# A two-step graph attention layer: the first step's guess kept as a logarithm, its last arithmetic moved from VectorE to ScalarE and GpSimd

## The chip, the cores and the metric

The kernel runs on one core of a Trainium2 chip. A core has five engines with queues of their own: TensorE (PE in the profile, with its weight loads as PEld), VectorE (DVE), ScalarE (ACT), GpSimd (POOL) and SyncE (SP), which here only issues transfers. The metric is the device time of one launch in microseconds.

## The reference, cut to what matters

`x` is 3327 x 256, `adj` is a sparse 3327 x 3327 matrix (about 0.12% of its entries and the diagonal), all float32.

```python
def _top_p_attention(X, W1, W2, W3):
    logits = (X @ W1.T @ W2.T) @ (X @ W3.T).T
    probs = softmax(logits, axis=-1)
    # sort each row downward; keep an entry while the sum before it is under 0.9
    keep_sorted = cs - sp < TOP_P
    A = probs * mask
    return A / A.sum(-1)

h = relu(layernorm(x))
R = rownorm(adj + I)
Z, Xf, Xa = 0, h, h
for n in range(2):
    A = _top_p_attention(Xa, W1, W2, W3)
    Xf = R @ Xf
    Xa = A @ Xa
    Z = Z + Xf @ U1[n].T + Xa @ U2[n].T
out = x + layernorm(h + Z) * ln_g + ln_b
```

So each of the two steps forms 3327 rows of 3327 attention weights, cuts from each row the smallest entries that make up the last tenth of its sum, and multiplies what is left by the node features. Beside it runs the sparse product with `R`.

## The kernel before

**Tiles and slots.** The rows are split into 26 tiles of 128. Each step is a loop over slots, one tile each (`for i in range(-1, NT + 2)`); a slot has seven parts (`PARTS`). What is issued in each part is written out by hand as strings in `PLAN`, `BEGIN`, `OPEN` and `LAST`: each letter advances one generator to its next `yield`. At the end dependencies are added that hold PE, ACT, DVE and POOL to the order of the program text, so the text is the queue of each engine.

**The way of a tile through the first step.** `weights` (letters w, q) makes a row block of logits on PE and its exponentials on ACT (lines 600 to 610). `measured_once` (letter m) guesses, for each row, a value a little above the cut: a few operations on one column per row on ACT and POOL (lines 620 to 646), two scans of all 3328 entries on ACT (line 633: a sum of Relu and a sum of Sign against a first guess), then seven one-column operations on ACT (lines 653 to 659) and five on DVE (lines 662 to 666), the last of which writes the guess, column 16. `settle` (letters d, c) then takes one DVE pass over the row block that keeps what is under the guess (line 724, "the w pass" below), searches the largest 40 of these with MAX8 and MATCH_REPLACE8 (lines 732 to 751), and takes a second DVE pass that writes zeros under the cut found (line 761, "the e pass"). `Sums` transposes the block on PE (line 810), copies it from PSUM on ACT (line 812) and multiplies it by the features on PE (line 824). Column 16 only has to be close: `prove` checks afterwards that each row's cut is exact, and where one isn't, the whole layer is computed again by `search_graph_layer`, a slower kernel in the same program.

**The sparse product.** `listed` (letter a) reads `adj` and finds for each row block which of the column blocks hold anything (lines 854 to 863); the first four of a row go into `index` directly, the rest are counted on DVE into `over` (line 866) and packed: `packed` (letter p) multiplies the counts by a triangular matrix on PE (line 876), copies the result on ACT (line 877) and makes a 128 x 128 selection of zeros and ones with two DVE operations (lines 880 and 881); `gathered` (letter h) multiplies by it (line 887) and writes the fifth index (lines 889 to 895). With these indices POOL issues ten indirect transfers per tile, five of `adj` blocks (line 901) and five of feature rows (line 922). Letter g issues one of the ten; each is made to follow the ACT instruction that stands last before it in the text. `spread` (letter s) is the product on PE (line 930). `first_end` (letter e) ends a tile's first step: a transposition, a product with `U2`, and on POOL the sum of line 947, `sv`.

**Queues around the change.** POOL's queue in a slot of the first step holds, in this order from the w pass on: the rest of the feature gathers (line 922), `index` of line 895, five operations of `project` (lines 541 to 545), in every other slot line 502, one `adj` gather and the sum of line 907, lines 643 to 646 of the guess, then line 922, four of line 901 with `index` of line 864 among them, and the sum of line 947. DVE's queue holds the w pass, the MAX8 work with the reductions of `listed` in between, lines 880 and 881, the e pass, line 763, line 894, lines 662 to 666, line 538, and the next w pass.

Of the kernel before, what the change touches and what calls it, by code (L numbers as in the profile page):

```python
# [9 lines left out]
F32 = mybir.dt.float32  # L10
# [3 lines left out]
AF = mybir.ActivationFunctionType  # L14
ALU = mybir.AluOpType
# [3 lines left out]
P = 128  # L19
# [4 lines left out]
NP = NT * P  # L24
# [288 lines left out]
BIG = 1.0e30  # L313
# [3 lines left out]
ROUNDS = (5, 5)  # L317
PG = (0.72168716, 3.51308980, -3.48705157)
PK = (3.57528079, -2.54929187, 0.86603878)
OFFSET = (18.0, 24.0)  # L320
TOPK = 8 * max(ROUNDS)
LNY = 0.25 * math.log(0.72)

SQG, SQK = ((c[0], c[1] / (2 * c[0]), c[2] - c[1] ** 2 / (4 * c[0])) for c in (PG, PK))
# [12 lines left out]
DIRECT = 4  # L337
LIST = 16
# [7 lines left out]
def guess_graph_layer(ctx, tc, x, adj, w1t, w2t, w3t, u1t, u2t, ln_g, ln_b, out, flag):  # L346
    nc = tc.nc

    const = ctx.enter_context(tc.tile_pool(name="const", bufs=1))
# [6 lines left out]
    small = ctx.enter_context(tc.tile_pool(name="small", bufs=4))  # L356
# [5 lines left out]
    V, G, S, PE = nc.vector, nc.gpsimd, nc.scalar, nc.tensor  # L362

    rows_of = lambda t: min(P, N - t * P)
    valid = lambda t: 0 <= t < NT
# [44 lines left out]
    for k, c in enumerate((-0.5, 0.5, -1.0, -0.5)):  # L410
        G.memset(half[:, k : k + 1], c)
    law = const.tile([P, 7, NT], F32, tag="law", name="law")
    one = const.tile([P, 8], F32, tag="one", name="one")
    for k, c in enumerate((1.0, -1.0, 5.0e-4, SQG[1], SQK[1], math.log(10.0), LNY, 1.0e-12)):
        G.memset(one[:, k : k + 1], c)
    of_s = const.tile([P, 4], F32, tag="of_s", name="of_s")
    for k, c in enumerate((SQG[0], SQG[2], -SQK[0], -SQK[2])):
# [14 lines left out]
    place = const.tile([P, P], F32, tag="place", name="place")  # L432
# [5 lines left out]
    lists = const.tile([P, NT, LIST + 1], F32, tag="lists", name="lists")  # L438
    over = const.tile([P, NT], F32, tag="over", name="over")
# [188 lines left out]
    def con(k):  # L628
        return one[:, k : k + 1]
# [5 lines left out]
    def measured_once(r):  # L635
        e, ms = r["e"], r["ms"]


        col = guessed(r, small.tile([P, 17], F32, tag="g", name="g"))
        S.activation(col(4), col(2), AF.Square, bias=con(4))  # L640
        S.activation(col(11), col(4), AF.Identity, scale=ms(5), bias=ms(6))
        S.activation(col(1), col(0), AF.Exp, scale=-1.0, bias=con(5))
        G.tensor_scalar(col(7), col(9), 0.5, None, ALU.mult)
        G.tensor_scalar(col(8), col(9), 0.5 * NP, None, ALU.mult)
        G.tensor_scalar(col(5), col(1), OFFSET[0], None, ALU.mult)
        G.tensor_scalar(col(10), col(9), col(5), 1.0, ALU.mult, ALU.add)
        yield
        oa = small.tile([P, 3], F32, tag="oa", name="oa")
        through(e, AF.Relu, col(9), -1.0, oa[:, 0:1])
        yield  # L650
        through(e, AF.Sign, col(9), -1.0, oa[:, 1:2])
        yield
        S.activation(col(3), oa[:, 0:1], AF.Identity, scale=-1.0, bias=col(8))
        S.activation(col(4), oa[:, 1:2], AF.Relu, scale=col(7), bias=col(3))
        S.activation(col(6), col(4), AF.Ln, scale=col(1), bias=con(2))
        S.activation(col(3), col(4), AF.Square, scale=col(1), bias=con(1))
        S.activation(col(3), col(3), AF.Ln, scale=0.5, bias=col(10))
        S.activation(col(3), col(3), AF.Identity, scale=-1.0, bias=col(6))
        S.activation(col(3), col(3), AF.Exp, scale=col(11))
        yield  # L660

        V.tensor_scalar(col(5), oa[:, 1:2], NP - 31.0, BIG, ALU.is_gt, ALU.mult)
        V.tensor_scalar(col(6), col(4), col(1), 0.35, ALU.mult, ALU.is_lt)
        V.scalar_tensor_tensor(col(5), col(6), BIG, col(5), ALU.mult, ALU.add)
        V.tensor_scalar(col(3), col(3), 1.0e20, col(9), ALU.min, ALU.mult)
        V.tensor_tensor(col(16), col(3), col(5), ALU.add)

    def measured_twice(r):
        e, ms = r["e"], r["ms"]
# [6 lines left out]
        G.tensor_scalar(col(11), col(11), ms(5), ms(6), ALU.mult, ALU.add)  # L676
        G.tensor_scalar(col(5), col(1), OFFSET[1], None, ALU.mult)
        G.tensor_scalar(col(7), col(3), ms(3), ms(8), ALU.mult, ALU.add)
# [33 lines left out]
    def measured(step, r):  # L712
        return measured_twice(r) if step else measured_once(r)
# [123 lines left out]
    def listed():  # L837
        pieces = [(t, j0, min(size, NT - j0)) for t in range(NT) for size in (HALF if t < HALVES else AD,)
                  for j0 in range(0, NT, size)]

        def asked(t, j0, n):
            at = (roomy[(2 * t + j0 // HALF) % 4] if t < HALVES else
                  adjp.tile([P, AD, P], F32, tag="at", name="at", bufs=2))
            nc.sync.dma_start(at[:, :n], adj[t, :, j0 : j0 + n, :])
            return at

        ahead = asked(*pieces[0])
        for k, (t, j0, n) in enumerate(pieces):
            at = ahead
            if k + 1 < len(pieces):  # L850
                ahead = asked(*pieces[k + 1])
            if j0 == 0:
                fm = small.tile([P, NT], F32, tag="fm", name="fm", bufs=2)
            V.tensor_reduce(fm[:, j0 : j0 + n], at[:, :n], AX.X, ALU.max, apply_absolute_value=True)  # L854
            if j0 + n < NT:
                yield
                continue
            V.scalar_tensor_tensor(fm, fm, 0.0, back, ALU.is_gt, ALU.mult)
            V.memset(fm[:, t : t + 1], 0.0)
            ls = lists[:, t, :]  # L860
            V.max(ls[:, :8], fm)
            V.match_replace(fm, ls[:, :8], fm, 0.0)
            V.max(ls[:, 8:LIST], fm)
            G.tensor_scalar(index[:, t, :DIRECT], ls[:, :DIRECT], -1.0, float(NONE), ALU.mult, ALU.add)
            of = small.tile([P, LIST], F32, tag="of", name="of", bufs=2)
            V.tensor_scalar(of[:, DIRECT:], ls[:, DIRECT:LIST], 0.0, None, ALU.is_gt, ALU.add,
                            accum_out=over[:, t : t + 1])
            done.append(t)
            yield

    def packed(t):

        assert t in done
        ls, ov = lists[:, t, :], over[:, t : t + 1]
        pb = ps_t.tile([P, 4, P], F32, tag="pt", name="pb")
        PE.matmul(pb[:, 0, :1], upto, ov, start=True, stop=True)
        S.copy(ls[:, LIST:], pb[:, 0, :1])
        yield
        ohs[t] = oh = small.tile([P, P], F32, tag="oh", name="oh", bufs=2)
        V.tensor_scalar(oh, place, ov, ls[:, LIST:], ALU.subtract, ALU.is_lt)  # L880
        V.scalar_tensor_tensor(oh, place, ls[:, LIST:], oh, ALU.is_ge, ALU.mult)

    def gathered(t):
        oh = ohs.pop(t)
        ls, n = lists[:, t, :], LIST - DIRECT
        po = ps_t.tile([P, 4, P], F32, tag="pt", name="po")
        PE.matmul(po[:, 0, : n + 1], oh, ls[:, DIRECT:], start=True, stop=True)
        lo = small.tile([P, n], F32, tag="lo", name="lo", bufs=2)
        S.copy(lo, po[:, 0, :n])
        nth = small.tile([P, 1], F32, tag="nth", name="nth")  # L890
        S.activation(nth, po[:, 0, n : n + 1], AF.Identity, scale=-1.0, bias=part)
        yield
        of = small.tile([P, LIST], F32, tag="of", name="of", bufs=2)
        V.scalar_tensor_tensor(of[:, :n], place[:, :n], nth, lo, ALU.is_equal, ALU.mult, accum_out=nth)
        G.tensor_scalar(index[:, t, DIRECT:], nth, -1.0, float(NONE), ALU.mult, ALU.add)

    def adjacent(t):
# [83 lines left out]
        V.tensor_copy(flag, pf[:1, 0, :1])  # L981

    own_of = {}
    live, ohs, acs, xgs, done, early = {}, {}, {}, {}, [], {}
    none = iter(())

    def run(work, n=99):
# [42 lines left out]
    for q in range(HALF + 5):  # L1030
        if 0 <= q - 3 < HALF:
            k, pk = q - 3, made.pop(q - 3)
# [17 lines left out]
        if 0 <= q - 2 < HALF:  # L1050
            k, pt = q - 2, turned.pop(q - 2)
# [10 lines left out]
        if 0 <= q - 1 < HALF:  # L1062
            k, rn = q - 1, scaled.pop(q - 1)
            pt = ps_t.tile([P, 4, P], F32, tag="pt", name="pt")
            for h in range(2):
                t = 2 * k + h
# [4 lines left out]
        if 0 <= q - 4 < HALF and 2 * (q - 4) in COUNTED:  # L1071
            k = q - 4
# [54 lines left out]
    def refetch(t):  # L1127
# [6 lines left out]

    PLAN = (("gmdsssa", "gmcdsssa", "edawwpg", "gmsdga", "gmspdea", "ohgdawwqg", "gehmgq"),
            ("llcmssg", "lnmsg", "lwwnfdgg", "lcmdsss", "fdsmwqdf", "llmd", "lmwfdg"))

    LAST = {NT - 1: ("cfss", "cn", "nd", "sss", "fddddddsf", "f", ""), NT: ("c", "", "", "ff", "ff", "fv", "f"),  # L1140
            NT + 1: ("fv", "f", "", "", "f", "f", "f")}
    BEGIN = {-1: ("mba", "mmbba", "mwwbbaa", "bmwwb", "", "", ""),
             0: ("mdbb", "mcdbb", "medbwwbp", "mdbb", "gmpdbwwb", "hgdbgbq", "hgq"),
             1: ("ggmdsssbb", "gmcdgsssbb", "gedbwwbp", "bmsdg", "gmpdeg", "hgdwwqg", "hgemgqo"),
             2: ("gmdsssa", "gmcdsssga", "gedawwpg", "gmsdga", "gmspdea", "ohgdawwqg", "gehmgq")}
    OPEN = {-1: ("llcmss", "lnms", "lwwnfd", "lcmdsssggggg", "fmgdswqdf", "llmdf", "lmwfdm"),
            0: ("cmssggg", "nms", "wwnfd", "cmdsss", "fdsmgwqdf", "mdf", "mwd"),
            1: ("cmss", "nms", "wwnfd", "cmdsssgggg", "fdsmwqdf", "mgd", "mwfdg")}
# [9 lines left out]
    for step in range(2):  # L1158
        sums = Sums(step, live, xw if step else x0, AHEAD[step])

        for i in range(-1, NT + 2):
# [4 lines left out]
            if step == 1 and i == -1:  # L1166
# [6 lines left out]
                c=work["d"],  # L1173
# [25 lines left out]
            for k in range(PARTS):  # L1199
                g = PARTS * (i - 1) + k - LATE[step]  # L1200
                summing = valid(g // PARTS)
                if step and valid((g + AHEAD[1]) // PARTS):
                    sums.turn(g + (k == 2), min(i, NT - 1))
                for c in ({**OPEN, **LAST} if step else BEGIN).get(i, PLAN[step])[k]:
                    at = len(trace)
# [76 lines left out]
```

## Time and profile before

| | us |
|---|---|
| median of 3 runs | 1366.73 |
| lowest and highest of the runs | 1366.65 to 1367.74 |
| the profiled execution, its time | 1366.65 |
| its span (first to last instruction) | 1364.9 |
| beginning, up to the first slots | 0 to 136 |
| slots of the first step | 136 to about 680 |
| between the steps | 680 to 760 |
| slots of the second step | 760 to 1365 |

The span is 1.75 us shorter than the execution's time; the granted TensorE clock is 0.984 of full speed over the whole span, and 1.00 in the slots of the first step from 209 to 618 us. In the page, a group's line gives line, engine, operation, output and inputs, shapes and count, then the busy time of the group, the mean of one in ns, and the idle time before them with what ended it. In the timeline each line is a start, a duration, an engine and an instruction.

### The profile page before, as it was taken

How to read it: one execution, taken by the hardware profiler on the slowest of the kernel's cores; microseconds unless marked ns; L12 is line 12 of the kernel's file. 1: busy time of each engine (PE TensorE's matmuls, PEld its weight loads, DVE VectorE, ACT ScalarE, POOL GpSimd, SP SyncE). 2: the span in 40 equal slices, each digit the busy share in tenths (PEclk: the TensorE clock that was granted, in tenths of full speed). 3: DMA queues.
4: the chain of work that ended last, by engine and by line, in shares of the span. 5: the costliest groups of instructions: out<-in, count | busy, mean ns of one | idle time of the engine just before them, and what ended most of it. 6: DMA issues, size and time to landing. Idle time of an engine off the chain costs nothing.

```text
span 1364.9 us, 22101 instructions
## 1 busy us (share of the span) xinstructions
PE 1267.0 (93%) x6495; PEld 973.5 (71%) x6495; DVE 1150.7 (84%) x3455; ACT 1072.4 (79%) x2342; POOL 1048.0 (77%) x1425
## 2 busy tenths in 40 slices
PE   5989999999999999999999499999998999999985
PEld 4535778777787877778786277767676767676775
DVE  6877999999999999999973788787878787878793
ACT  5466788889888888888844898898979898989851
POOL 5215888888888888888872788888888888888872
PEclk9989999999999999999999699999999999999998
DMA  8734454454545455453532222212221312122200
GB/s 293 223 117 136 132 162 130 142 158 129 160 133 148 138 144 150 138 160 107 146 89 85 62 75 65 78 61 80 66 74 50 90 50 90 58 82 65 75 24 23
DMA packets 92642, 149.77 MB, mean 110 GB/s; under 512 B 15425, under 2 KB 59072, under 8 KB 92512
## 3 DMA queue, kind: packets, MB, share of 16 engines
q1 hardware_dynamic: 75056, 105.37, 24.6%
q0 software_dynamic: 16640, 42.69, 11.9%
q8 instruction: 54, 0.88, 0.3%
q14 instruction: 76, 0.62, 0.1%
q10 hardware_dynamic: 816, 0.20, 0.1%
HBM read 120.93 MB, written 27.28 MB: 109 GB/s over the span
## 4 chain that ended last, share of the span: by engine, by line
DVE 47%; PE 24%; POOL 16%; ACT 6%; issue 5%; DMA 1%; POOLq 0%; SPq 0%; DVEq 0%; ACTq 0%
DVE e L761 9%; DVE cand L732 8%; PE pa L824 7%; DVE w L724 6%; POOL xg L922 6%; PE pl L600 5%; DVE fm L854 5%; DVE bb L739 3%; PE pt L810 3%; DVE cand L741 3%; PE pr L930 3%; ACT ja L633 3%; PE pz L1012 2%; DVE x L761 2%; POOL s L970 1%
## 5 line engine op out<-in xcount | busy, mean ns | idle before, releaser
L824 PE MATMUL pa<-xw,eT 128*128 128x256 f32 x1352 | 322.6, 383 | 4.2 <-DVE s L954 2.3
L633 ACT ACTIVATE ja<-e,g 128x3328 uint8<-128x3328 f32 x106 | 325.9, 3074 | 0.1
L824 PE MATMUL pa<-x,eT 128*128 128x256 f32 x1352 | 322.0, 379 | 0.0
L824 PEld LDWEIGHTS pa<-xw,eT 128*128 128x128 f32 x1352 | 249.8, 190 | 53.3 <-issue 14.4
L824 PEld LDWEIGHTS pa<-x,eT 128*128 128x128 f32 x1352 | 242.8, 190 | 25.5
L732 DVE MAX8 cand<-w 128x8 f32<-128x168 f32 (+1 forms) x1040 | 253.4, 317 | 0.0
L922 POOL DMA_INDIRECT xg<-bx,index x130 | 202.2, 1555 | 50.8 <-issue 23.4
L812 ACT COPY eT<-pt 128x512 f32<-128x512 f32 (+1 forms) x364 | 200.2, 557 | 43.0 <-PE pt L810 42.8
L810 PE MATMUL pt<-ident,e 128*128 128x128 f32 x1144 | 176.2, 276 | 29.9 <-DVE e L761 18.3
L901 POOL DMA_INDIRECT ac<-in_adj,index x130 | 148.9, 1145 | 59.0 <-ACT e L1018 16.5
L810 PEld LDWEIGHTS pt<-ident,e 128*128 128x128 f32 x1144 | 139.3, 144 | 73.6 <-issue 44.3
L724 DVE SCALAR_TENSOR_TENSOR w<-e,g 128x3328 f32<-128x3328 f32 x44 | 163.7, 3720 | 2.6 <-ACT g L709 2.5
L922 POOL DMA_INDIRECT xg<-vx,index x130 | 134.6, 1035 | 40.6 <-issue 24.6
L761 DVE SCALAR_TENSOR_TENSOR e<-e,rec 128x3328 f32<-128x3328 f32 x40 | 151.7, 3792 | 0.6
L930 PE MATMUL pr<-xg,ac 128*128 128x257 f32 (+1 forms) x520 | 140.5, 394 | 8.2 <-DVE s L1120 6.5
L604 ACT ACTIVATE e<-pl 128x832 f32<-128x832 f32 x132 | 113.1, 861 | 28.6 <-PE pl L600 25.8
L930 PEld LDWEIGHTS pr<-xg,ac 128*128 128x128 f32 x520 | 93.7, 194 | 34.7 <-issue 15.0
L600 PE MATMUL pl<-both,qT 64*128 64x416 f32 x416 | 93.0, 546 | 7.7 <-ACT e L604 4.3
L600 PE MATMUL pl<-after,qT 64*128 64x416 f32 x416 | 97.2, 562 | 0.2 <-ACT e L604 0.2
L739 DVE MAX8 bb<-cand 128x8 f32<-128x160 f32 x260 | 84.3, 324 | 5.5
L466 POOL TENSOR_TENSOR rstd<-rstd,half 128x1 f32<-128x1 f32 x26 | 84.1, 3236 | 2.2
L854 DVE TENSOR_REDUCE fm<-at 128x4 f32<-128x512 f32 (+1 forms) x133 | 84.3, 634 | 0.6 <-DMA at<-in_adj 0.6
(258 smaller groups left out, 2140.9 us busy)
## 6 DMA issues: line engine op xcount, KB each, us to landing
at<-in_adj SPq DMA_DIRECT2D x114, 256.0 KB
cx<-ac SPq DMA_DIRECT2D x26, 384.0 KB
ac<-cx SPq DMA_DIRECT2D x26, 384.0 KB
wide<-in_adj SPq DMA_DIRECT2D x8, 832.0 KB
e<-in_adj SPq DMA_DIRECT2D x6, 832.0 KB
own<-bx SPq DMA_DIRECT2D x26, 128.5 KB
x<-in_x SPq DMA_DIRECT2D x13, 256.0 KB
xr<-in_x SPq DMA_DIRECT2D x26, 128.0 KB
```

The lines of the kernel that those rows point to most:

```text
L600: PE.matmul(pl[:, a, :wd], qT[p, :], keys_of(step, a).rearrange("p a b -> p (a b)")[:, c : c + wd], start=True, stop=True)
L633: S.activation(ja, e, f, bias=guess, scale=sign, accum_out=total)
L724: V.scalar_tensor_tensor(w, e, col(16), e, ALU.is_lt, ALU.mult, accum_out=d2)
L732: V.max(cand[:, 8 * s : 8 * s + 8], w[:, s * SEG : min(NP, (s + 1) * SEG)])
L761: V.scalar_tensor_tensor(e, e, at(1), e, ALU.is_ge, ALU.mult, accum_out=ra)
L810: PE.transpose(pt[:, j, :], e[:, (j0 + j) * P : (j0 + j + 1) * P], ident)
L812: S.copy(eT[:, :w, :], pt[:, :w, :])
L824: PE.matmul(self.pa, eT[:, c - 4 * k, :], self.xa[:, j, :], start=c == 0, stop=c == NT - 1)
L854: V.tensor_reduce(fm[:, j0 : j0 + n], at[:, :n], AX.X, ALU.max, apply_absolute_value=True)
L901: G.indirect_dma_start(out=ac[:, k, :], out_offset=None, in_=rows, in_offset=bass.IndirectOffsetOnAxis(ap=index[:, t, k : k + 1], axis=0), ...
L922: G.indirect_dma_start(out=xg[:, k, :w], out_offset=None, in_=rows, in_offset=bass.IndirectOffsetOnAxis(ap=index[:, t, k : k + 1], axis=0))
L930: PE.matmul(pr[:, :w], ac[:, k, :], own if k == KT - 1 else xg[:, k, :w], start=k == 0, stop=k == KT - 1)
```

## The change

The change touches the first step's guess and the packing of indices; the numbers of search rounds stay (5, 5).

- The guess of the first step is worked out as a logarithm. Four POOL operations on one column are added in the first part of `measured_once` (a sign change, two for a constant less the logarithm of the first guess, 0.035 of the row's sum). On ACT a Square leaves the seven operations after the scans, and two of the seven, now a Relu and an Exp, stand behind three DVE operations in a fifth part of the generator, which is issued in part 5 of the slot, ahead of the e pass, where before five DVE operations stood at the slot's end. The two guards that before added 1e30 to the guess now take 60 from the term under the Relu. The constant in the logarithm goes from 18 to 19.
- The count of the blocks beyond the first four moves from a DVE operation in `listed` to a Sign with a sum on ACT, in a new function `counted`, with two new one-column POOL operations. It is issued two tiles ahead, in `gathered`.
- In `packed`, one of two DVE operations on 128 x 128 remains; a one-column Identity and a 128 x 128 Square on ACT are added.

```diff
-OFFSET = (18.0, 24.0)
+OFFSET = (19.0, 24.0)
@@ measured_once
         S.activation(col(1), col(0), AF.Exp, scale=-1.0, bias=con(5))
+        G.tensor_scalar(col(11), col(11), -1.0, None, ALU.mult)
         G.tensor_scalar(col(7), col(9), 0.5, None, ALU.mult)
         G.tensor_scalar(col(8), col(9), 0.5 * NP, None, ALU.mult)
         G.tensor_scalar(col(5), col(1), OFFSET[0], None, ALU.mult)
         G.tensor_scalar(col(10), col(9), col(5), 1.0, ALU.mult, ALU.add)
+        G.tensor_scalar(col(12), col(3), ms(3), ms(8), ALU.mult, ALU.add)
+        G.tensor_scalar(col(12), col(12), -1.0, 80.0, ALU.mult, ALU.add)
+        G.tensor_scalar(col(13), r["Z"], 0.035, None, ALU.mult)
         yield
...
         S.activation(col(6), col(4), AF.Ln, scale=col(1), bias=con(2))
-        S.activation(col(3), col(4), AF.Square, scale=col(1), bias=con(1))
-        S.activation(col(3), col(3), AF.Ln, scale=0.5, bias=col(10))
-        S.activation(col(3), col(3), AF.Identity, scale=-1.0, bias=col(6))
-        S.activation(col(3), col(3), AF.Exp, scale=col(11))
-        yield
-
-        V.tensor_scalar(col(5), oa[:, 1:2], NP - 31.0, BIG, ALU.is_gt, ALU.mult)
-        V.tensor_scalar(col(6), col(4), col(1), 0.35, ALU.mult, ALU.is_lt)
-        V.scalar_tensor_tensor(col(5), col(6), BIG, col(5), ALU.mult, ALU.add)
-        V.tensor_scalar(col(3), col(3), 1.0e20, col(9), ALU.min, ALU.mult)
-        V.tensor_tensor(col(16), col(3), col(5), ALU.add)
+        S.activation(col(10), col(10), AF.Ln)
+        S.activation(col(10), col(10), AF.Identity, scale=-1.0, bias=col(6))
+        yield
+        V.tensor_scalar(col(5), oa[:, 1:2], NP - 31.0, 60.0, ALU.is_gt, ALU.mult)
+        V.tensor_scalar(col(14), col(4), col(13), 60.0, ALU.is_lt, ALU.mult)
+        V.scalar_tensor_tensor(col(12), col(12), col(5), col(14), ALU.subtract, ALU.subtract)
+        S.activation(col(10), col(10), AF.Relu, scale=col(11), bias=col(12))
+        S.activation(col(16), col(10), AF.Exp, scale=-1.0, bias=con(8))
@@ listed
-            of = small.tile([P, LIST], F32, tag="of", name="of", bufs=2)
-            V.tensor_scalar(of[:, DIRECT:], ls[:, DIRECT:LIST], 0.0, None, ALU.is_gt, ALU.add,
-                            accum_out=over[:, t : t + 1])
+    def counted(t):
+
+        if t not in done or t in nhs:
+            return
+        of = small.tile([P, LIST], F32, tag="of", name="of", bufs=2)
+        ov = over[:, t : t + 1]
+        S.activation(of[:, DIRECT:], lists[:, t, DIRECT:LIST], AF.Sign, accum_out=ov)
+        nhs[t] = nh = small.tile([P, 3], F32, tag="nh", name="nh", bufs=4)
+        G.tensor_scalar(nh[:, 0:1], ov, -0.5, 0.5, ALU.mult, ALU.add)
+        G.tensor_scalar(nh[:, 1:2], ov, ov, 0.25, ALU.mult, ALU.mult)
@@ packed
         S.copy(ls[:, LIST:], pb[:, 0, :1])
-        yield
+        S.activation(nh[:, 2:3], pb[:, 0, :1], AF.Identity, scale=-1.0, bias=nh[:, 0:1])
         ohs[t] = oh = small.tile([P, P], F32, tag="oh", name="oh", bufs=2)
-        V.tensor_scalar(oh, place, ov, ls[:, LIST:], ALU.subtract, ALU.is_lt)
-        V.scalar_tensor_tensor(oh, place, ls[:, LIST:], oh, ALU.is_ge, ALU.mult)
+        S.activation(oh, place, AF.Square, bias=nh[:, 2:3])
+        yield
+        V.tensor_scalar(oh, oh, nh[:, 1:2], None, ALU.is_lt)
@@ gathered
         V.scalar_tensor_tensor(of[:, :n], place[:, :n], nth, lo, ALU.is_equal, ALU.mult, accum_out=nth)
+        if valid(t + 2):
+            counted(t + 2)
         G.tensor_scalar(index[:, t, DIRECT:], nth, -1.0, float(NONE), ALU.mult, ALU.add)
@@ the plan of the first step, part 5 (likewise in BEGIN)
-    PLAN = (("gmdsssa", "gmcdsssa", "edawwpg", "gmsdga", "gmspdea", "ohgdawwqg", "gehmgq"),
+    PLAN = (("gmdsssa", "gmcdsssa", "edawwpg", "gmsdga", "gmspdea", "ohgmdawwqg", "gehmgq"),
```

More of the change, by code (lines that the diff above doesn't have):

```diff
@@ L412, in guess_graph_layer @@
     law = const.tile([P, 7, NT], F32, tag="law", name="law")
-    one = const.tile([P, 8], F32, tag="one", name="one")
-    for k, c in enumerate((1.0, -1.0, 5.0e-4, SQG[1], SQK[1], math.log(10.0), LNY, 1.0e-12)):
+    one = const.tile([P, 9], F32, tag="one", name="one")
+    for k, c in enumerate((1.0, -1.0, 5.0e-4, SQG[1], SQK[1], math.log(10.0), LNY, 1.0e-12, 80.0)):
         G.memset(one[:, k : k + 1], c)
@@ L864, in listed @@
             G.tensor_scalar(index[:, t, :DIRECT], ls[:, :DIRECT], -1.0, float(NONE), ALU.mult, ALU.add)
-            of = small.tile([P, LIST], F32, tag="of", name="of", bufs=2)
-            V.tensor_scalar(of[:, DIRECT:], ls[:, DIRECT:LIST], 0.0, None, ALU.is_gt, ALU.add,
-                            accum_out=over[:, t : t + 1])
             done.append(t)
             yield
+    def counted(t):
[7 more added lines that the diff above has]
+        G.tensor_scalar(nh[:, 1:2], ov, ov, 0.25, ALU.mult, ALU.mult)
     def packed(t):
-        assert t in done
+        counted(t)
+        nh = nhs[t]
         ls, ov = lists[:, t, :], over[:, t : t + 1]
@@ L877, in packed @@
         S.copy(ls[:, LIST:], pb[:, 0, :1])
+        S.activation(nh[:, 2:3], pb[:, 0, :1], AF.Identity, scale=-1.0, bias=nh[:, 0:1])
+        ohs[t] = oh = small.tile([P, P], F32, tag="oh", name="oh", bufs=2)
+        S.activation(oh, place, AF.Square, bias=nh[:, 2:3])
         yield
-        ohs[t] = oh = small.tile([P, P], F32, tag="oh", name="oh", bufs=2)
-        V.tensor_scalar(oh, place, ov, ls[:, LIST:], ALU.subtract, ALU.is_lt)
-        V.scalar_tensor_tensor(oh, place, ls[:, LIST:], oh, ALU.is_ge, ALU.mult)
+        V.tensor_scalar(oh, oh, nh[:, 1:2], None, ALU.is_lt)
     def gathered(t):
@@ L983, in guess_graph_layer @@
     own_of = {}
-    live, ohs, acs, xgs, done, early = {}, {}, {}, {}, [], {}
+    live, ohs, acs, xgs, done, nhs, early = {}, {}, {}, {}, [], {}, {}
     none = iter(())
@@ L1142, in guess_graph_layer @@
     BEGIN = {-1: ("mba", "mmbba", "mwwbbaa", "bmwwb", "", "", ""),
-             0: ("mdbb", "mcdbb", "medbwwbp", "mdbb", "gmpdbwwb", "hgdbgbq", "hgq"),
-             1: ("ggmdsssbb", "gmcdgsssbb", "gedbwwbp", "bmsdg", "gmpdeg", "hgdwwqg", "hgemgqo"),
-             2: ("gmdsssa", "gmcdsssga", "gedawwpg", "gmsdga", "gmspdea", "ohgdawwqg", "gehmgq")}
+             0: ("mdbb", "mcdbb", "medbwwbp", "mdbb", "gmpdbwwb", "hgmdbgbq", "hgq"),
+             1: ("ggmdsssbb", "gmcdgsssbb", "gedbwwbp", "bmsdg", "gmpdeg", "hgmdwwqg", "hgemgqo"),
+             2: ("gmdsssa", "gmcdsssga", "gedawwpg", "gmsdga", "gmspdea", "ohgmdawwqg", "gehmgq")}
     OPEN = {-1: ("llcmss", "lnms", "lwwnfd", "lcmdsssggggg", "fmgdswqdf", "llmdf", "lmwfdm"),
```

## Prediction

> **What bounds the kernel now.** I read the page first: busy shares, then the slices.
>
> ```profile
> PE 1267.0 (93%) x6495; PEld 973.5 (71%) x6495; DVE 1150.7 (84%) x3455; ACT 1072.4 (79%) x2342; POOL 1048.0 (77%) x1425
> PE   5989999999999999999999499999998999999985
> DVE  6877999999999999999973788787878787878793
> POOL 5215888888888888888872788888888888888872
> ```
>
> Slices 5 to 19 are the first step, where the change lies: PE and DVE at nine tenths, POOL only at eight. So POOL seems to have room. The stretch from one w pass to another, 17 slots later, gives the slot: 409.01 / 17 = 24.06 us.
>
> ```profile
> 209.07:618.08 409.01, 407.33 (x2171) 322.74 (x2171) 394.68 (x1226) 346.13 (x857) 347.99 (x398) 1.00 0.50 144
> ```
>
> Its columns after the length are PE, PEld, DVE, ACT, POOL. PE is idle for 1.68 us in 17 slots, 0.10 a slot. DVE is idle 0.84 a slot, which its timeline shows as hundredths between short instructions. The waits of this stretch:
>
> ```profile
> POOL xg L922 <- issue: 16.3, 55, 0.4
> POOL ac L901 <- issue: 7.4, 32, 0.3
> PE pt L810 <- DVE e L761: 1.6, 5, 0.5
> ```
>
> PE waits 1.6 us in all for DVE's e pass; DVE waits for nobody. POOL's rows are all 0.2 to 0.5 us long: the step before each gather. So what is POOL's idle fifth? One slot of DVE, then of POOL:
>
> ```profile
> 401.39 3.68 DVE L724 SCALAR_TENSOR_TENSOR w<-e,g 128x3328 f32<-128x3328 f32 x1
> ...
> 420.04 4.16 DVE L761 SCALAR_TENSOR_TENSOR e<-e,rec 128x3328 f32<-128x3328 f32 x1
> ...
> 425.07 0.14 DVE L662 TENSOR_SCALAR g<-oa 128x1 f32<-128x1 f32 x1
> ...
> 425.76 0.22 DVE L538 SCALAR_TENSOR_TENSOR mq<-mq 128x65 f32<-128x65 f32 x1
> ...
> 425.91 3.68 DVE L724 SCALAR_TENSOR_TENSOR w<-e,g 128x3328 f32<-128x3328 f32 x1
> ```
>
> ```profile
> 299.22 0.73 POOL L947 TENSOR_TENSOR sv<-sv,x 128x256 f32<-128x256 f32 x1
> ...
> 401.69 4.20 POOL L922 DMA_INDIRECT xg<-bx,index  x1 [0.30 <-issue]
> 406.20 0.95 POOL L922 DMA_INDIRECT xg<-bx,index  x1 [0.30 <-ACT xa L833]
> ...
> 412.68 0.26 POOL L643 TENSOR_SCALAR g<-g 128x1 f32<-128x1 f32 x1
> 413.00 0.21 POOL L644 TENSOR_SCALAR g<-g 128x1 f32<-128x1 f32 x1
> 413.29 0.21 POOL L645 TENSOR_SCALAR g<-g 128x1 f32<-128x1 f32 x1
> 413.61 0.26 POOL L646 TENSOR_SCALAR g<-g 128x1 f32<-128x1 f32 x1
> 414.27 1.02 POOL L922 DMA_INDIRECT xg<-bx,index  x1 [0.40 <-issue]
> ...
> 419.62 0.99 POOL L901 DMA_INDIRECT ac<-in_adj,index  x1 [0.27 <-ACT nth L891]
> 420.64 4.14 POOL L947 TENSOR_TENSOR sv<-sv,x 128x256 f32<-128x256 f32 x1
> 424.94 0.98 POOL L922 DMA_INDIRECT xg<-bx,index  x1 [0.16 <-issue]
> ```
>
> A POOL instruction that starts inside one of DVE's two long passes stands still until the pass is over: a gather takes 4.20 us instead of 0.95, `sv` 4.14 instead of 0.73 (its row at 299.22). That is 3.24 + 3.41 = 6.65 us lost in a slot. Between these two POOL goes from instruction to instruction without a stop. So a slot of POOL is 24.06 - 6.65 = 17.4 us of its own work and dispatch, and the lost part; it is as full as PE and DVE, and that is the fact on which I build. It keeps step because the loss gives way a little: what POOL loses in a pass is the pass (3.68) plus the 0.83 after it until a caught gather ends (405.07 to 405.90), less the gather's own 0.96, less the time into the pass at which it started, its cover: 3.55 - cover. Here the cover of the w pass is 0.30. The most is a gather started just ahead of the pass and the step after it, 0.97 + 0.30 = 1.27, a loss of 2.28.
>
> **The change, part by part.**
>
> *DVE.* Gone per slot are the count of line 866 (416.45, next start 0.09 later), one of lines 880 and 881 (0.37 between their starts), and two of five guess operations (five take 0.69, 425.07 to 425.76). About 0.7 us less. The three that stay move ahead of the e pass, so the way from the e pass's end (424.20) to the next w pass shrinks from 1.71 to 1.01.
>
> *PE.* Nothing is added or removed. DVE's gain is worth only what PE waits: 0.10 to 0.2 a slot, so 23.9.
>
> *ACT.* Added: a Sign with a sum on 128 x 12 (nearest row, line 620: 0.33 with its readout), an Identity on one column (line 891: 0.27), a 128 x 128 Square (between the copy of line 528, 0.26, and the 256 wide activation of line 1067, 0.59; I take 0.4): 1.0 us. The seven guess operations stay seven. In the slot from 401 to 425 ACT stands 1.40, 0.57, 1.12 and 0.62 us waiting for PE, and these cover it. Gone, it would cost up to 1.0 a slot. The last two guess operations wait for DVE, and behind them on ACT stand the exponentials of line 604; in this slot ACT waits there for PE until 420.19 anyway, as long as DVE comes to them by then.
>
> *POOL.* Six one-column operations more a slot: four in the guess, two for the count. Starts of lines 643 to 646 lie 0.31 apart, so 1.86 us; by the nearest extremes (line 544 to 545, 0.18; 542 to 543, 0.36) 1.1 to 2.2. I take 1.86, from the same kind of operation. POOL's work becomes 17.4 + 1.86 = 19.3, and a slot of it 19.3 plus the losses: 23.8 with both covers at most, 26.4 with none.
>
> What is late next: lines 643 to 646 slip. DVE's second guess operation needs column 13, the last of the eight POOL operations. Call the first one's start X. The eight end at X + 2.5; two DVE operations follow (0.45), then the e pass, at X + 3.0. Today it comes 7.36 after X (412.68 to 420.04), so POOL may fall back 4.4 us; by 19.3 + 6.65 - 23.9 = 2.0 a slot that is used up after about two slots. From then on POOL sets the pace. Its gathers after the eight start at X + 2.9 and X + 4.15; the second is 1.15 into the e pass, loses 2.4, and ends at X + 7.5. The next would start at X + 7.8; the w pass begins at X + 3.0 + 3.68 + 1.01 = X + 7.7, just ahead of it: cover 0.1, loss 3.45. A slot: 19.3 + 2.4 + 3.45 = 25.1. Were the w pass 0.15 later, the cover would be 1.25 and the slot 24.0. In 6 of 21 slots the end of `listed` stands between the passes (303.45 to 306.17), the w pass comes at X + 8.7, cover 0.4: 24.8. I take it as it falls: 15 at 25.1, 6 at 24.8, mean 25.0, 0.95 above today.
>
> The sum, on the profiled execution (1366.65, 0.08 under the median): slots of tiles 3 to 23 less two for the fall back, some 19 x 0.95 = 18; the two at -0.2; total 1384. The second step is not touched and the beginning has shorter queues: nothing, within 2 us either way.
>
> The Trainium skill says in SBUF — State Buffer, section "Who interferes with whom", that a two-input VectorE operation without a two-port mode takes only the pair's read interface, and infers that descriptor generation, needing the write interface, is not held by it. The row above (4.20 beside 0.95) differs, and the measurement decides. By the page's inference only `sv` would lose time, POOL would have some 3 us free, and the result would be that of the first rival below. Perfetto Trace Analysis, section "Optimizing Scalar/DVE Operations", warns that moving work between VectorE and GpSimd might not help, since they share a port; that goes with my sum.
>
> **The rivals.**
>
> *POOL fits, PE sets the pace (faster).* The new operations cost 0.18 apart (1.1 us) and the covers settle high: 17.4 + 1.1 + 4.6 = 23.1, under PE's 23.9. For it: DVE's 0.7 is real, and the phase has settled by itself so far. Against it: today's covers, 0.3 mostly. 21 x -0.16: 1363.
>
> *It cancels.* 1.86 with both covers at most: 23.8 to 24.1, between 1363 and 1368, say 1366.
>
> *ACT stalls on top.* While POOL is late, ACT waits for column 8 and then for DVE; its cover of 3.7 us is used up and its 1.0 us counts too: 21 x 1.0 on 1384, 1405. Against it: in a longer slot it has more room.
>
> *The guess misses.* The dropped Square makes the guess a little different; one row whose cut isn't among the 40 runs the slow kernel. That is 27 scans for each of 52 tiles, at 3.07 + 0.20 (line 633) 4.6 ms more. Against it: 18 becomes 19 to make up for it, and the rest is the same formula as a logarithm.
>
> **How the numbers follow.** Forecast (POOL sets a slot of 24.4 to 25.6): 0.68, its own range 1373 to 1397. POOL fits: 0.15. Cancels: 0.08. ACT on top: 0.07. Misses: 0.02. Time 1384. For 8 in 10 the range reaches down to the first rival and up past the dear end (2.2 us, 19 x 1.55 = 29): 1363 to 1400. A change of 0.2%, 2.7 us, is about the least that a measurement tells from none. Faster 0.15; same 0.08; slower 0.77.
>
> **What would show it.** Right: a first-step slot near 25 us; DVE waiting at line 664 for POOL, ACT at line 657; PE idle 1 us a slot; POOL still without a stop, `g` operations 0.3 apart. Wrong: POOL's rows with real waits, slots at 23.9, or a gather caught at the very end of its run in both passes.

## The result and the profile after

The changed kernel takes 1407.2 us (median of 4 runs, 1406.78 to 1412.55), the kernel before 1366.7 (1365.16 to 1367.74): ratio 1.0306, interval 1.028 to 1.0333. The profiled execution has a span of 1405.3 us, 40.4 more than before. The page's busy shares and three rows of its slices:

```profile
PE 1280.2 (91%) x6495; PEld 971.4 (69%) x6495; DVE 1125.2 (80%) x3325; ACT 1086.1 (77%) x2446; POOL 1083.4 (77%) x1582
PE   5989999999999999999989679999998999999986
DVE  6777798888988988979862588778787878788794
POOL 5216888888888888887863588888888888888872
```

DVE has lost most of its nines in the first step; POOL is still at eight, though it is now what ends last. The stretch over the same 17 slots, from one w pass to another (length, PE, PEld, DVE, ACT, POOL):

```profile
212.94:645.23 432.29, 416.65 (x2174) 319.60 (x2173) 378.43 (x1145) 355.25 (x924) 370.46 (x500) 1.00 0.47 136
```

A slot is 25.43 us where it was 24.06, and PE is idle 0.92 us in each. PE was to be idle 1 us a slot by the forecast. Waits of this stretch (in total, times, longest), the first two rows and the first of SP's own:

```profile
DVE fm L855 <- DMA at<-in_adj: 41.4, 17, 4.1
ACT g L657 <- POOL g L648: 33.4, 17, 2.6
```

```profile
SPq L962 <- POOL sv L960: 165.5, 15, 12.4
```

DVE, which waited for nobody, now waits 2.4 us a slot for the tiles `at` of the adjacency; ACT waits 2 us a slot for the sixth of the eight POOL operations of the guess; POOL has no row of a real stop; SP holds the store `sx <- sv` for POOL's sum, 165.5 us in 15 times. One slot of POOL, cut, and DVE's two passes in it:

```profile
388.71 4.38 POOL L914 DMA_INDIRECT ac<-in_adj,index  x1 [0.30 <-ACT of L875]
...
404.53 0.26 POOL L643 TENSOR_SCALAR g<-g 128x1 f32<-128x1 f32 x1
...
406.58 0.21 POOL L650 TENSOR_SCALAR g<-rec 128x1 f32<-128x1 f32 x1
...
409.94 4.04 POOL L914 DMA_INDIRECT ac<-in_adj,index  x1 [0.30 <-issue]
414.29 4.37 POOL L914 DMA_INDIRECT ac<-in_adj,index  x1 [0.31 <-issue]
```

```profile
398.36 0.69 DVE L855 TENSOR_REDUCE fm<-at 128x4 f32<-128x512 f32 x1 [2.55 <-DMA at<-in_adj]
...
409.49 3.68 DVE L762 SCALAR_TENSOR_TENSOR e<-e,rec 128x3328 f32<-128x3328 f32 x1
...
414.17 3.68 DVE L725 SCALAR_TENSOR_TENSOR w<-e,g 128x3328 f32<-128x3328 f32 x1
```

The w pass starts at 414.17 and the next gather at 414.29, 0.12 later: it is caught at the very beginning and takes 4.37 us. Of the 18 w passes from that of tile 4 on, 13 have a gather that starts 0.12 or 0.13 into them and takes 4.37 or 4.38.

Where the 40.5 us arise is read from the starts of the w and e passes in both traces. I use this measure below: the *shift* of a pass is its start in one kernel less that in the kernel before, each from its one profiled execution.

| pass | shift, us | since the row above |
|---|---|---|
| w pass, tile 4 | 4.2 | the beginning: 4.2 |
| w pass, tile 24 | 28.9 | 20 slots: 24.7 |
| e pass, tile 24 | 36.8 | 7.9 |
| first w pass of the second step | 40.5 | 3.7 |
| from there to the end of the second step | 40.5 | 0 |

### The profile page after: what moved, and what is told of

It is laid out like the page before. It is cut to its first block, busy times and chain, and to the rows that moved or that the text cites. A ratio compares the mean times of both kernels' runs of the same rounds, so it can differ in the third digit from the quotient of the medians.

```text
span 1405.3 us, 22255 instructions
## 1 busy us (share of the span) xinstructions
PE 1280.2 (91%) x6495; PEld 971.4 (69%) x6495; DVE 1125.2 (80%) x3325; ACT 1086.1 (77%) x2446; POOL 1083.4 (77%) x1582
## 3 DMA queue, kind: packets, MB, share of 16 engines
q1 hardware_dynamic: 75056, 105.37, 23.8%
q0 software_dynamic: 16640, 42.69, 11.3%
## 4 chain that ended last, share of the span: by engine, by line
PE 33%; POOL 24%; DVE 19%; ACT 14%; issue 7%; DMA 2%; SPq 0%; POOLq 0%; ACTq 0%; DVEq 0%
PE pa L825 11%; POOL xg L935 9%; PE pl L600 6%; PE pt L811 5%; ACT ja L633 4%; PE pr L943 4%; DVE e L762 4%; DVE cand L733 2%; PE pz L1025 2%; DVE x L762 2%; POOL ac L914 2%; DVE bb L740 2%; DVE w L725 2%; DVE cand L742 1%; PE pz L956 1%
## 5 line engine op out<-in xcount | busy, mean ns | idle before, releaser
L633 ACT ACTIVATE ja<-e,g 128x3328 uint8<-128x3328 f32 x106 | 325.1, 3067 | 0.1
L914 POOL DMA_INDIRECT ac<-in_adj,index x130 | 258.7, 1990 | 52.6 <-issue 15.4
L811 PE MATMUL pt<-ident,e 128*128 128x128 f32 x1144 | 177.3, 278 | 34.1 <-DVE e L762 17.7
L935 POOL DMA_INDIRECT xg<-bx,index x130 | 137.8, 1060 | 45.4 <-issue 21.8
L762 DVE SCALAR_TENSOR_TENSOR e<-e,rec 128x3328 f32<-128x3328 f32 x40 | 147.3, 3683 | 0.6
```

The costliest lines, as they stand in the source:

```text
L633: S.activation(ja, e, f, bias=guess, scale=sign, accum_out=total)
L762: V.scalar_tensor_tensor(e, e, at(1), e, ALU.is_ge, ALU.mult, accum_out=ra)
L811: PE.transpose(pt[:, j, :], e[:, (j0 + j) * P : (j0 + j + 1) * P], ident)
L914: G.indirect_dma_start(out=ac[:, k, :], out_offset=None, in_=rows, in_offset=bass.IndirectOffsetOnAxis(ap=index[:, t, k : k + 1], axis=0), ...
L935: G.indirect_dma_start(out=xg[:, k, :w], out_offset=None, in_=rows, in_offset=bass.IndirectOffsetOnAxis(ap=index[:, t, k : k + 1], axis=0))
```

## The experiments

Slots in this table are means from the w pass of tile 4 to that of tile 22 (the change has 25.33 by this measure, the kernel before 24.06). *Loss* is what POOL's instructions take above their usual time (a gather 0.95, the sum 0.75) because they were caught in one of DVE's passes, *own* the rest of the slot, POOL's work and dispatch; waits of POOL over 0.6 us stand apart.

| kernel | POOL operations added | own | loss | slot | us | ratio and interval |
|---|---|---|---|---|---|---|
| before | 0 | 17.74 | 6.32 | 24.06 | 1366.7 | |
| e11_three_idle | 3 | 18.42 | 5.59 | 24.00 | 1369.1 | 1.0016, 0.9996 to 1.0036 |
| e3_six_idle | 6 | 19.39 | 5.97 | 25.37 | 1388.9 | 1.0160, 1.0135 to 1.0184 |
| e12_twelve_idle | 12 | 20.68 | 5.76 | 26.44 | 1422.6 | 1.0416, 1.0400 to 1.0432 |
| the change | 6 | 19.22 | 6.11 | 25.33 | 1407.2 | 1.0306, 1.0280 to 1.0333 |
| e1_guess_only | 4 | 18.48 | 6.47 | 24.94 | 1394.5 | 1.0198, 1.0173 to 1.0224 |
| e2_count_only | 2 | 18.17 | 5.99 | 24.20 | 1376.6 | 1.0074, 1.0051 to 1.0096 |
| e4_store_later | 6 | 19.01 | 5.86 | 24.86 | 1400.6 | 1.0255, 1.0231 to 1.0279 |
| e7_other_column | 6 | | | 25.28 | 1406.4 | 1.0293, 1.0272 to 1.0315 |
| e8_old_place | 6 | | | 25.01 | 1401.6 | 1.0249, 1.0228 to 1.0271 |
| e9_old_ends | 6 | | | 25.24 | 1404.1 | 1.0280, 1.0264 to 1.0296 |
| e5_count_act | 0 | 17.52, waits 0.49 | 5.77 | 23.78 | 1367.7 | 1.0006, 0.9991 to 1.0021 |
| e6_none_on_pool | 0 | 17.48, waits 0.81 | 5.50 | 23.80 | 1374.5 | 1.0060, 1.0041 to 1.0080 |
| e10_act_and_old_ends | 0 | | | 23.78 | 1366.2 | 0.9987, 0.9972 to 1.0003 |

**The two halves.** One has the lines of `counted`, `packed` and `gathered` as before, the other `measured_once`, the plan and OFFSET as before.

> The changed kernel with the counting and packing of indices put back as it was before: only the guess as a logarithm stays, with four of the six POOL operations. Theory (POOL's queue and its two caught stretches set the slot): four operations at 0.31 us make a POOL slot of 17.4 + 1.24 + 2.4 + 3.4 = 24.5 us, so slots of 24.3 to 25.0 and, over 19 slots, 1373 to 1390 us; the 6.3 us in which DVE waits at the end of the first step for ACT's selection and ACT for POOL's count are gone. Rival (the count's new chain DVE, ACT, POOL, ACT, DVE is the cause): slots of 24.1 or less and 1362 to 1370.

> The changed kernel with the guess put back as it was before (seven ACT operations, five on DVE at the slot's end, four POOL operations fewer): only the counting and packing stay, with two more POOL operations. Theory (POOL's queue sets the slot): 17.4 + 0.62 + 6.65 = 24.7 at today's covers, 24.0 if they give way; slots of 24.0 to 24.6, and some 7 us more at the end of the first step from the chain through POOL's count: 1370 to 1386. Rival (the guess's new hop is the cause): 1364 to 1369, no waits at the end.

The halves add up: 29.2 and 11.3 us above 1365.3, the kernel before as it was measured beside them, 40.5 together. The count alone came as expected. The guess alone has the slot of the theory (24.94) but is 4.5 us above its range of times: its shift is already 9.6 at the w pass of tile 4, a loss at the beginning that the range did not hold.

**POOL's length alone.** The kernel before, with

```
+        G.tensor_scalar(idle(0), col(11), -1.0, None, ALU.mult)
         G.tensor_scalar(col(7), col(9), 0.5, None, ALU.mult)
...
+        G.tensor_scalar(idle(2), r["Z"], 0.035, None, ALU.mult)
...
+        G.tensor_scalar(idle(4), part, part, 0.25, ALU.mult, ALU.mult)
         G.tensor_scalar(index[:, t, DIRECT:], nth, ...)
```

and three more of the kind; nobody reads what they write. Later the same with half and with twice as many.

> The kernel before with six POOL operations added at the places where the change adds them; nothing reads what they write, and nothing else is changed. Theory (length of POOL's queue alone): slots of 24.8 to 25.6, 1380 to 1398. Rival (the moved DVE and ACT work and the new waits make the loss, POOL has room): 1364 to 1370.

> The kernel before with three idle one-column POOL operations a slot (two in the guess, one at the end of a slot) and nothing else. Theory (POOL's own 17.4 + 3 x 0.31 and the losses in DVE's passes, which give way by up to half a microsecond as in the counting alone): slot 24.3 to 24.7 us, 1370 to 1378 us. Rival (POOL has room until some point and then jumps): slot under 24.15, 1365 to 1368 us.

> The kernel before with twelve idle one-column POOL operations a slot and nothing else. Theory (from six on the covers are used up, each further operation costs its 0.31 us): slot 27.0 to 27.4 us, 1422 to 1432 us. Rival (the covers of DVE's passes still give way, as between none and six): slot 26.4 or less, 1400 to 1415 us.

Six idle operations give the slot of the change, 25.37 beside 25.33, with no other part of the change present. So the loss in the slots is POOL's length. Part of it may come by way of SP's queue, of which more below: with the six idle operations DVE waits for `at` as it does in the change (`DVE fm L860 <- DMA at<-in_adj: 21.2, 16, 2.4` from 213 to 640 us), with three it does not. The other two missed: three cost no slot time at all (24.00, the rival's case, the time 1 us above its range), since the losses in the passes give way by 0.73; twelve cost 1.07 a slot more than six where 1.86 was expected: the time is at the low end of the theory's range, the slot at the high end of the rival's. The column of own work says where the difference lies: an operation costs 0.23, 0.27 and 0.25 us of POOL in the three, not the 0.31 between starts of lines 643 to 646.

**The other side: nothing on POOL.** In the count, its two operations go to ACT:

```
-        G.tensor_scalar(nh[:, 0:1], ov, -0.5, 0.5, ALU.mult, ALU.add)
-        G.tensor_scalar(nh[:, 1:2], ov, ov, 0.25, ALU.mult, ALU.mult)
+        S.activation(nh[:, 0:1], ov, AF.Identity, scale=-0.5, bias=half[:, 1:2])
+        S.activation(nh[:, 1:2], ov, AF.Square, scale=0.5)
```

and in e6 also those of the guess:

```
-        G.tensor_scalar(col(11), col(11), -1.0, None, ALU.mult)
-        G.tensor_scalar(col(12), col(3), ms(3), ms(8), ALU.mult, ALU.add)
-        G.tensor_scalar(col(12), col(12), -1.0, 80.0, ALU.mult, ALU.add)
-        G.tensor_scalar(col(13), r["Z"], 0.035, None, ALU.mult)
+        S.activation(col(12), col(3), AF.Identity, scale=ms(3), bias=ms(8))
+        S.activation(col(13), r["Z"], AF.Identity, scale=0.035)
...
```

The two operations that only turn a sign and subtract from 80 are not replaced: three DVE operations and one of ACT are written with the other sign instead.

> The counting and packing of the change alone, its two one-column operations done on ACT instead of POOL (each 0.2 to 0.3 us); the guess as before; POOL's queue as long as before. POOL theory: with nothing added to POOL the first-step slot is back at 23.9 to 24.1 us and the end of the first step loses the wait of ACT for POOL's late operation, so 1362 to 1369 us. Rival (it is the new chain DVE, ACT, PE, ACT, DVE of the packing that costs, whoever does the two operations): 1373 to 1379, as the counting alone with them on POOL (1376.6).

> The whole change with nothing added to POOL: the count's two operations, the logarithm of the cut and the scaled sum of the row on ACT, the negation and the second of the two operations of the offset dropped by turning signs (the cap on the guess is the same 80). ACT gets some 1 us a slot more than in the change. POOL theory: slot 23.8 to 24.2 us; of the losses outside the slots the one at the beginning (gathers behind the end of the guess, 4) stays and the one at the end shrinks to 0 to 7, so 1365 to 1379 us. Rival (ACT's added work and its waits for DVE cost as much as POOL's): slot over 24.8, 1388 or more.

Both times lie in the ranges of the theory of POOL, and the slot of e5 is 0.12 us under its range. The stretch of 17 slots in e6:

```profile
215.14:620.15 405.01, 405.01 (x2164) 321.05 (x2163) 379.86 (x1147) 364.50 (x988) 332.65 (x399) 1.00 0.50 145
```

PE is busy for all of 405.01 us: 23.82 a slot is what PE needs here. POOL now has real waits (`POOL ac L912 <- ACT ja L633: 10.1, 9, 1.3` among the waits of this stretch). ACT does 0.5 us a slot more than in the change (364.50 beside 355.25) and the slot is 23.80. That is ACT's cover with POOL in time; for the case with POOL late it is e3 that speaks: ACT does there what it did before, and the slot is that of the change. So ACT is no cause of the slower slots. Of the 40.5 us above the kernel before 7.7 are left (1374.5 beside the 1366.8 of the kernel before as measured with it), and PE's instructions are the same.

**The waits named by the trace.** ACT's wait for line 648 is a write-after-read: line 657 writes column 3, which the added line 648 still reads. And the store `sx <- sv` stands in SP's queue, which the program holds to the order of its text in the first step too, waits there for POOL's sum, and the loads of `at` stand behind it.

```
-        S.activation(col(3), oa[:, 0:1], AF.Identity, scale=-1.0, bias=col(8))
-        S.activation(col(4), oa[:, 1:2], AF.Relu, scale=col(7), bias=col(3))
+        S.activation(col(15), oa[:, 0:1], AF.Identity, scale=-1.0, bias=col(8))
+        S.activation(col(4), oa[:, 1:2], AF.Relu, scale=col(7), bias=col(15))
```

> The change with line 657 writing column 15 instead of column 3, which the added POOL operation of line 648 still reads: ACT then waits for column 8 (three POOL operations earlier) and not for line 648. Theory (POOL's own length sets the slot, and ACT's wait only shows how late POOL is): slot within 0.3 us of 25.33, 1401 to 1408 us. Rival (the wait of ACT, 2.6 us each time, is itself on the chain that sets the slot): slot 24.7 or less, 1388 to 1398 us.

```
+        sent()
         sv = row.tile([P, D], F32, tag="sv", name="sv", bufs=2)
...
+        unsent.append((t, sv))
         yield
-        nc.sync.dma_start(sx[t], sv)
```

> The changed kernel with the store of line 962 (sx from sv) issued one slot later in SP's queue, so that the loads of adj behind it do not wait for POOL's sum. Theory (POOL's queue sets the slot): the 2 to 4 us per slot that DVE waits for adj go, POOL still runs without a stop, slots stay at 24.6 to 25.3 and the time at 1395 to 1407. Rival (the store ahead of the loads on SP sets the slot: POOL's sum, store, load, reduction, e pass, w pass, POOL): slots of 24.2 or less, 1375 to 1388.

In e7 ACT waits for line 645 instead, 17.7 us where it was 33.4, and the time stays: that wait only shows how late POOL is. In e4 DVE's waits for `at` are gone and the slot is 0.47 shorter; what takes their place:

```profile
ACT g L657 <- POOL g L648: 36.2, 16, 2.6
...
DVE g L664 <- ACT g L658: 14.3, 15, 1.0
...
DVE g L663 <- POOL g L647: 12.2, 16, 2.0
```

DVE now waits for POOL's operations of the guess directly: line 663 overwrites column 5, which line 647 on POOL still reads. It also waits for line 658, which stands behind ACT's own wait for POOL. SP's queue was worth 5 to 7 us: the medians differ by 6.6, and by 5.2 when each is taken from the kernel before as measured beside it.

**The beginning and the end.** e8 puts the end of the guess back to the slot's end (the plan's rows as before). e9 leaves the change as it is, but tiles that were not counted two ahead are packed on DVE:

```
     def packed(t):
-        counted(t)
+        if t not in nhs:
...
+            V.tensor_scalar(of[:, DIRECT:], ls[:, DIRECT:LIST], 0.0, None, ALU.is_gt, ALU.add, accum_out=ov)
...
+            return
         nh = nhs[t]
```

> The change with the end of the guess (three DVE and two ACT operations) issued where it was before, at the slot's end behind the fifth part. Theory of the beginning: gathers no longer stand behind the last ACT operation of the guess, the shift of the beginning (4.2 us at the seventh w pass) falls under 1.5; the slots stay at 25.0 to 25.6 since POOL sets them; 1399 to 1406 us. Rival (the place also sets the slot, by DVE's wait for column 13 ahead of the e pass): slot 24.7 or less and 1385 to 1397. Other rival: the old place puts 0.7 us of DVE between e pass and w pass again and nothing else, 1407 to 1415.

> The change, but a tile whose list wasn't counted two tiles ahead (the last one, and those ahead of the first slots) is counted and packed on DVE as before. Theory (the loss at the end of the first step is the last tile's chain from DVE's list over ACT's Sign, POOL's late operation and ACT's square back to DVE, on which the e pass of tile 24 stands): the jump of 7.9 us between the w pass and the e pass of that tile falls under 1.5, the rest stays: 1397 to 1403 us. Rival (POOL's backlog meets the end of the step whatever the packing does): the jump stays over 5, 1404 to 1410 us.

The jump at the last tile is settled. Rows of the change's waits from 655 to 800 us:

```profile
ACT nh L888 <- POOL nh L877: 7.9, 2, 7.0
...
DVE oh L892 <- ACT oh L890: 6.3, 1, 6.3
```

The list of the last tile comes too late to be counted ahead, so its whole chain (DVE's list, ACT's sign, POOL's operation behind 7 us of queue, ACT's square, DVE's comparison) stands on the path, and with it the e pass of tile 24. In e9 that step of the shift is 0.9 where the change has 7.9, the theory's case. It is not POOL's queue alone: in e6, where the chain goes over ACT, the step is still 4.6. The profile taken of e9, of a run of 1400.4 us, has 5.8 us less shift at the second step; its median is only 3.1 below that of the change, 1.1 above the range I gave and in that of the rival. In the profile its shift at the w pass of tile 4 is 7.2, 3.0 more than in the change.

The last 3.7 of the table are not explained by this chain. From the w pass of tile 25 to the second step's first PE is idle 8.0 us in the change and before, but busy 70.39 with 362 instructions where it was 66.31 with 338: PE had that much more left to do behind DVE. With three idle operations alone it is 69.58 with 357. Where PE fell behind is not shown.

The beginning went against me: e8's shift at the w pass of tile 3 is 10.3, not under 1.5; its time is in the range I gave, but because its slot is 25.01; why the slot is 0.32 shorter than in the change is not shown. Of the 10.3, 3.7 are there at its first w pass already, which stands ahead of the edited part of the slot (the profiled run is 4.0 us above the median of e8); without them 6.6 are left. DVE's waits from 108 to 172 us, in the change and in e8:

```profile
DVE g L663 <- ACT ja L633: 2.8, 2, 2.2
...
DVE g L664 <- ACT g L658: 1.9, 2, 0.9
```

```profile
DVE w L725 <- ACT g L666: 2.7, 1, 2.7
...
DVE w L725 <- ACT g L667: 0.8, 1, 0.8
```

In the first slots ACT's scans are late. In the new place DVE's operations wait for them, and for line 658 behind them, ahead of the e pass, 4.7 us; in the old place the w pass waits for the last two operations that now follow on ACT, 3.5. The kernel before has none of these rows. The change's longest row here is another, for the packing (`DVE oh L892 <- ACT oh L890: 5.6, 2, 3.4`, before 2.7); e9 has the packing of the first tiles as before and keeps the shift. At the w pass of tile 3 the seven kernels with the new guess have shifts of 4.6 to 10.3, the six others 0.0 to 2.4, whether twelve operations were added to POOL (2.3) or none (e6: 7.7). Counted from each kernel's first w pass it is 4.3 to 7.9 and -1.4 to 0.6. So the beginning belongs to the guess; that the waits above are all of it is not shown, and which of its orders would cost nothing was not tried.

**Towards a better kernel.** e5 with the packing of e9:

> The counting alone with its two operations on ACT, and the tiles not counted ahead packed on DVE as before. Theory: the slots stay at 23.8 us (0.28 under those of before, 5 us in 18), and the loss of 4.2 us between the end of the first step and the second goes: 1361 to 1365 us, some 3 to 5 under before. Rival (the 4.2 us come from elsewhere, and PE's pace decides the end too): 1366 to 1369, as the counting on ACT alone (1367.7).

1366.2 beside 1366.3, the rival's range; its ratio's interval holds 1. The slots keep their 0.28, and the shift at the w pass of tile 22 is -5.3, but at the first w pass of the second step -2.7: some is given back at the step's end. The profiled run is 2.4 us under the median, about as much, and the interval reaches 0.16% to either side. No kernel here is measurably faster than before.

## The prediction against the runs

Direction and mechanism were right, the time was not: 1384 with 1363 to 1400, and it is 1407.

- *What bounds.* That POOL is full, time stood still in DVE's passes included, holds: six idle operations on it cost 1.3 us a slot, and its removal leaves PE without a gap at 23.8 (predicted 23.9).
- *DVE.* Predicted 0.7 less a slot; busy fell by (394.68 - 378.43) / 17 = 0.96. Of this 0.26 is the e pass, which no edit touched: its 17 passes in the stretch take 62.72 us where they took 67.09 (4.16 for the one at 420.04, 4.72 at most, beside 3.68 now), and the forecast had counted 3.68 for it. Why it was longer before is not shown. The other 0.70 is the forecast. From the e pass's end to the w pass it is 1.00, as predicted (1.01). Worth nothing while POOL ends last, as said.
- *ACT.* Predicted 1.0 more and covered; busy rose 0.54, and e6 shows the cover. The rival of ACT on top named 1405, near the measured time, by a mechanism that is not there: e3 has the slot of the change (25.37 beside 25.33) without ACT's work. That its number was near is luck.
- *POOL's own.* 1.86 predicted, 1.48 measured (19.22 - 17.74, by the table's measure), inside the bounds of 1.1 and 2.2. The 17.4 was read from one slot that lost 6.65; the mean over the slots is 17.74 with 6.32. The loss was to be 2.4 and 3.45; it is 2.80 in the e pass and 3.31 in the w pass, and the gather stands 0.12 behind the w pass where 0.1 was read off. Own work came out 0.1 under the forecast's 19.3 and the loss 0.3 to 0.4 above it: 25.33 beside 25.0.
- *What is late next.* This step was half wrong. The e pass comes not at X + 3.0 but at X + 4.96 (404.53 to 409.49), and DVE stands not at line 664 for POOL but at the reductions for `at`. I had followed POOL's lateness through the columns of the guess and not through the store that SP holds back. Once SP is out of the way, in e4, DVE does wait for the guess on POOL, but at line 663 for line 647 (12.2 us in 16 times), not at line 664 for column 13.
- *The sum over the slots.* 19 slots at 0.95, 18 us; measured 24.7 over 20. This accounts for 6.7 of the 23 us by which the forecast fell short.
- *The step that failed.* "The second step is not touched and the beginning has shorter queues: nothing, within 2 us either way." The second step is untouched, but the way there is not: 4.2 us at the beginning and 11.6 after the last slots (7.9 at the last tile, 3.7 behind it), 15.8 that the sum had at nothing. I had costed the chain of the packing by its durations on engines with room, in the steady slot, where it is counted two tiles ahead. For the last tile there is no such lead, and e9 shows that the 7.9 come from it; for the first tiles ACT has no lead over DVE, which goes with the new guess in all seven kernels that have it. The 3.7 stay open.
- *POOL fits.* That rival is real, with another condition: at three added operations the losses give way by 0.73 and the slot stays at 24.00. At six it is past that point.

## What to carry to other kernels

An operation that is free in a steady loop needs its lead: look at the first and the last turns for the same chain, and add up what it costs where the lead is missing. Count as an engine's load what it stands still under another's long instructions, and when it falls behind, follow everything that waits for it, in-order DMA queues above all. Moving small operations to an engine with a low busy share can move the bound (POOL had 77%); the same operations on ACT (79%) cost no slot time here.

## What was not expected

A POOL operation of 0.2 us can be held like a gather when it starts just behind the beginning of DVE's pass: with twelve idle operations, the index operation that takes 0.24 us in the change (line 865 at 441.15) took as long as the e pass that began at 421.09:

```profile
420.04 1.03 POOL L936 DMA_INDIRECT xg<-bx,index  x1 [0.28 <-ACT xw L958]
421.14 3.68 POOL L874 TENSOR_SCALAR index<-lists 128x4 int32<-128x4 f32 x1
```

Not every one is: in e4 the same operation at 208.82, 0.02 us into an e pass, took 0.19. What decides it is not shown.

And the losses are no fixed tax: over the kernels of the table they moved between 5.5 and 6.5 us a slot, which hid three idle operations wholly, and six cost 1.3 us.
